# A graph transformer layer and a GAT layer: new start, constants as columns, last pair finished by quarters

## The chip, the cores and the metric

The kernel runs on one core of one Trainium2 chip. The metric is the device time of one execution in microseconds (us). A profiled execution gives a span, from the first to the last instruction, and the records of every engine. TensorE does matrix products into PSUM, VectorE and ScalarE work on rows of 128 partitions, GpSimd (POOL) does a few small operations, and SyncE (SP) issues most DMA transfers. Each engine takes its own instructions in order.

## The reference

There are 128 graphs (batches) of 128 nodes with 512 features, an adjacency matrix `adj` for each, and two layers, all in float32:

```
# layer 0: attention, 8 heads of 64
h = relu(layernorm(x))
q, k, v = h Wq^T + bq, h Wk^T + bk, h Wv^T + bv
attn = softmax((q k^T / 8) * (adj + adj))
x = x + (attn v) Wo^T + bo
# layer 1: graph attention
h = relu(layernorm(x))
Wh = h W ;  e = leaky_relu(Wh a1 + (Wh a2)^T, 0.2)
att = softmax(where(adj > 0.5, e, -9e15), axis=1)
x = x + elu(att Wh)
```

Here a1 and a2 are the two halves of the vector `a`.

## The kernel before

Graphs go in pairs: 64 pairs, numbered p from 0. Projections q, k and v are made for groups of two pairs (four graphs), and so one pair's steps carry half of the projection products of a later group. Every large product with a weight is written as seven smaller ones in place of eight (Winograd's form of Strassen's scheme): `PRODUCTS` lists, for each of the seven, the quarter of the activations, the quarter of the weights, and the PSUM bank (a, b or c). Weight tiles have seven slots: four quarters as loaded, and sums of quarters that `weight_sum` (steps Wv0 to Ww3) makes on VectorE. Products 0 and 1 use the loaded quarters 0 and 2; most others use sums. The token side has such sums too (`token_sum`: steps hs0 to hs3, cs, gs).

Work is divided into named steps, such as `lx` (load x of a pair), `t0`/`t1` (row statistics, lines 159 and 160), `pp` (reciprocal root on POOL, lines 163 and 164), `hn0`/`hn1` (normalised rows, line 181), `tp0`/`tp1` (turned by TensorE, line 188), `ev0`/`ev1` (ReLU into the hidden state, line 191), `U1` to `U11` (projection products, line 249), `F` and `A` (their evictions by ScalarE, lines 261 and 266, and additions by VectorE, line 270), `sca` to `plb` (scores, softmax, turned blocks that go out to memory and back), `o0` to `o6` and `w0` to `w6` (products with Wo and W, line 290), and `ez`, `fa`, `fb`, `so` (elu, addition, store: lines 476, 479, 482, 485). Three lists written out by hand give the order of the steps: `HEAD` for the first pairs, `ORDER` for each pair of the middle, `TAIL` for the last. Each list is one order over all engines; every engine takes its own instructions from it, in that order, DMA queues included. Pairs 0 to 3 turn their normalised rows on TensorE at the start; later pairs load x already transposed.

The first loads of `HEAD` are x of pair 0 in two halves, all of Wq (1 MB, `Lq`, line 622), x of pair 1, all of Wo and all of Wk. Before the lists begin, ScalarE's queue issues the biases bq, bk and bv as columns (`column`, line 107): 512 elements of 4 bytes each.

Two constants are made once. The row c is bo plus Wo applied to bv, minus 1, and is added to x of each pair (`sh`, line 225). It starts as a row bo that is spread over the partitions while it loads (`load_row`, line 120); `product_c` (line 494) makes the product with a broadcast column of bv on the one side and 256 columns of Wo on the other, so that the result stands on all partitions. The rows u_src and u_dst are W applied to a1 and a2: `dots_u` (line 507) makes columns by dot products on VectorE, `turn_u` spreads each with four transposes on TensorE, and `keep_u` copies it on ScalarE, u_src with the factor 1/MASK.

At the end, one exponential of 128x1024, two VectorE operations of 128x1024 and one store of 512 KB finish the last pair, as they do each pair.

Of the kernel before, what the change touches and what calls it, by code (L numbers as in the profile page):

```python
# [24 lines left out]
def kernel(  # L25
# [86 lines left out]
    bv_sb = column(bv, "bv")  # L112

# [3 lines left out]
    c_sb, us_sb, ut_sb = (const.tile([P, E], F32, name=name) for name in ("c", "u_src", "u_dst"))  # L117

    def load_row(dst, src, offset=0):
        nc.sync.dma_start(dst, bass.AP(tensor=src.tensor, offset=src.offset + offset, ap=[[0, P], [1, E]]))  # L120
# [32 lines left out]
    def row_stats(src, name):  # L153

        mv = small.tile([P, 2, 2], F32, name=name)

        def stats(i):
            st = small.tile([P, nc.vector.BN_STATS_DIM], F32, name="st")
            nc.vector.bn_stats(st, src[:, i, :])  # L159
            nc.vector.bn_aggr(mv[:, i, :], st)  # L160

        def power():
            nc.gpsimd.tensor_scalar_add(mv[:, :, 1], mv[:, :, 1], EPS)  # L163
            nc.gpsimd.tensor_tensor(mv[:, :, 1], mv[:, :, 1], mhalf.to_broadcast([P, 2]), OP.pow)  # L164

        return mv, stats, power
# [4 lines left out]
    def stats0(p, i):  # L171
        if p not in st0:
            st0[p] = row_stats(xs[p] if p < 3 else x0s[p], "mv0")
        st0[p][1](i)
# [234 lines left out]
    def dot1(p, i, k):  # L409
        h2, ws = h1s[p]  # L410
        junk = work.tile([P, E], F32, name="junk")
        nc.vector.scalar_tensor_tensor(  # L412
            junk, h2[:, i, :], 1.0, (us_sb, ut_sb)[k], op0=OP.mult, op1=OP.mult, accum_out=ws[:, i, k : k + 1]
        )
# [58 lines left out]
    def elu(p):  # L473

        ezs[p] = work.tile([P, 2, E], F32, name="ez")
        nc.scalar.activation(ezs[p], zs[p], AF.Exp)

    def finish_a(p):
        nc.vector.scalar_tensor_tensor(xs[p], zs[p], 0.0, xs[p], op0=OP.max, op1=OP.add)

    def finish_b(p):
        nc.vector.scalar_tensor_tensor(xs[p], ezs.pop(p), 1.0, xs[p], op0=OP.min, op1=OP.add)
# [4 lines left out]
    ucol = const.tile([P, 2, C], F32, name="ucol")  # L487


    def product_c():  # L490
        onces["c"] = pm = ps1.tile([P, 2, E // 2], F32, name="pm", tag="ps1")
        for f in range(2):
            for c in range(C):
                nc.tensor.matmul(  # L494
                    pm[:, f, :], bv_sb[:, c : c + 1].to_broadcast([P, P]), wo_sb[:, 2 * (c // 2) + f, c % 2, :],
                    start=(c == 0), stop=(c == C - 1),
                )

    def sum_c():
        pm = onces["c"].rearrange("p f k -> p (f k)")  # L500
        nc.vector.scalar_tensor_tensor(c_sb, pm, -1.0, c_sb, op0=OP.add, op1=OP.add)


    def dots_u(i, half):
        junk = work.tile([P, E], F32, name="junk")
        for c in (2 * half, 2 * half + 1):
            nc.vector.scalar_tensor_tensor(
                junk.rearrange("p (f k) -> p f k", f=2), w1_sb[:, 2 * half : 2 * half + 2, c % 2, :], 1.0,
                (us_sb, ut_sb)[i].rearrange("p (f k) -> p f k", f=2), op0=OP.mult, op1=OP.mult,
                accum_out=ucol[:, i, c : c + 1],  # L510
            )

    def turn_u(i):
        onces["u", i] = pu = ps1.tile([P, C, P], F32, name="pu", tag="ps1")
        for c in range(C):
            nc.tensor.transpose(pu[:, c, :], ucol[:, i, c : c + 1].to_broadcast([P, P]), ident)

    def keep_u(i):
        pu = onces["u", i].rearrange("p c k -> p (c k)")
        nc.scalar.activation((us_sb, ut_sb)[i], pu, AF.Copy, scale=1.0 if i else 1.0 / MASK)  # L520
# [11 lines left out]
    def listed(text, mark):  # L532
# [3 lines left out]
        lx@0 Lq@0 t0@-5 lx@1 Lo@0 Lk@0 Wq0@0 t1@-5 pp@0 t1@-4 lx@2 Lc@0 t0@-4 hn0@0 pp@1 Lv@0 hn1@0 tp0@0 Lw@0 tp1@0  # L536
        Lu0@0 ev0@0 hn1@1 ev1@0 hn0@1 tp1@1 Wq1@0 U6@-2 Wq2@0 tp0@1 ccp@0 ev0@1 t0@-3 F6@-2 t1@-3 ev1@1 Wk0@0 pp@2 l0@-2
        Wk2@0 la@-1 lt@0 Wk1@0 U5@-1 Lu1@0 hs2@-3 Wv0@0 hn0@2 U8@-2 ccd@0 hs0@-3 sh@0 U3@-1 t1@-2 tp0@2 F3@-1 la@0 U1@-1
        t0@-2 hs1@-3 pp@3 hn1@2 U7@-1 hs3@-3 hn0@3 hn1@3 U10@-2 cu01@0 F7@-1 l0@-1 ev0@2 Ww0@0 tp1@2 Wo0@0 U9@-1 ev1@2
        A8@-2 F10@-2 cu11@0 U1@-2 F9@-1 A5@-1 sh@1 tp0@3 U2@-1 tp1@3 F2@-1 U10@-1 ev0@3 A2@-1 ev1@3 hs0@-1 U4@-1 F10@-1  # L540
        Wv1@0 Wq3@0 t0@-1 U3@1 F4@-1 Ww1@0 hs1@-1 sca@0 t1@-1 scb@0 ata0@0 l0@0 s0@-1 ata1@0 U6@-1 mxa@0 Ww3@0 exa0@0
        U2@-2 Wv2@0 exa2@0 exa3@0 U8@-1 F1@-2 rca1@0 Wo2@0 nma2@0 exa1@0 U1@0 A9@-1 Wk3@0 rca0@0 t0@0 nma1@0 U3@-2
        nma3@0 A2@-2 nma0@0 t1@0 U4@-2 F3@-2 fla@0 l0@1 s0@0 f0@0 atb0@0 bla@0 U5@-2 atb1@0 Wv3@0 mxb@0 U11@-1 F5@-2
        exb3@0 U7@-2 A11@-1 exb1@0 A5@-2 exb0@0 cu00@0 U6@0 f0@1 pla@0 hs2@-1 Wo1@0 U2@0 F6@0 rcb0@0 A6@-1 F7@-2 exb2@0
        U9@-2 F1@0 rcb1@0 nmb3@0 F3@1 U10@0 A9@-2 lT@1 nmb2@0 cu10@0 nmb1@0 lT@0 sup0@0 scb@1 sua0@0 nmb0@0 sca@1 F10@0
        flb@0 U7@1 ata0@1 blb@0 ata1@1 A2@0 U5@1 F7@1 mxa@1 U9@1 Wo3@0 exa0@1 hd0@0 plb@0 exa2@1 exa1@1 pca@0 hs3@-1
        t0@1 U3@0 pea@0 rca0@1 hd1@0 nma1@1 exa3@1 U1@1 F3@0 rca1@1 t1@1 nma0@1 nma2@1 l0@2 s0@1 U2@1 nma3@1 la@1 fla@1
        U5@0 F2@1 atb0@1 bla@1 F9@1 hd0@1 o0@0 atb1@1 o1@0 mxb@1 pcb@0 pla@1 U4@1 peb@0 exb3@1 cs0@0 od0@0 exb1@1 cs1@0
        U8@0 A2@1 exb2@1 A5@1 exb0@1 cs2@0 U6@2 F5@0 A8@0 t0@2 t1@2 U4@0 od1@0 rcb1@1 rcb0@1 Ww2@0 nmb2@1 U8@1 nmb0@1
        nmb3@1 nmb1@1 U6@1 F4@1 flb@1 F6@2 hd1@1 U10@1 blb@1 hs0@1 cs3@0 o2@0 F10@1 A6@1 pca@1 od2@0 hs1@1 plb@1 sca@2  # L550
        pea@1 o4@0 ata0@2 ata1@2 o3@0 f0@2 od4@0 l0@3 mxa@2 U7@0 lt@1 od4c@0 A9@1 sup1@0 o5@0 sua1@0 exa1@2 o0@1 od5@0
        exa2@2 o1@1 exa0@2 o6@0 od0@1 st0@0 pcb@1 od6@0 st1@0 peb@1 scb@2 exa3@2 od1@1 pw@0 U11@1 cs0@1 rca1@2 rca0@2
        hs2@1 nma0@2 cs1@1 nma1@2 A5@0 s0@2 o2@1 nma2@2 nm@0 nma3@2 U1@2 F7@0 fla@2 h20@0 U9@0 atb0@2 F1@2 bla@2 h21@0
        atb1@2 mxb@2 U3@2 lT@2 A9@0 exb3@2 d00@0 exb2@2 U10@2 d01@0 pla@2 F3@2 od2@1 exb0@2 cs2@1 U5@2 hs3@1 A11@1 la@2
        d11@0 U4@2 F5@2 hd0@2 exb1@2 rcb1@2 rcb0@2 d10@0 o4@1 nmb3@2 nmb1@2 U8@2 od4@1 nmb2@2 A5@2 nmb0@2 flb@2 o3@1
        pb@0 U2@2 cs3@1 blb@2 od4c@1 wm@0 pr@0 U7@2 m1@0 o6@1 F7@2 plb@2 e1@0 o5@1 sw@0 U9@2 od6@1 hd1@2 g0@0 od5@1
        st0@1 g1@0 ge0@0 st1@1 A2@2
# [12 lines left out]
        so@-8 w0@-7 F10@-5 A9@-5 pw@-6 w1@-7 hs1@-5 sca@-4 zc0@-7 ge1@-7 scb@-4 ata0@-4 lx@-5 nm@-6 pca@-5 ata1@-4  # L570
        h21@-6 gs0@-7 mxa@-4 pcb@-5 pea@-5 U6@-4 peb@-5 A6@-5 exa1@-4 gs1@-7 gs2@-7 exa3@-4 cs0@-5 hs2@-5 o0@-5 h20@-6
        o1@-5 exa0@-4 d01@-6 U3@-3 exa2@-4 wd1@-7 cs2@-5 rca1@-4 d10@-6 nma3@-4 w2@-7 d00@-6 F6@-4 rca0@-4 U8@-4 sh@-5
        nma0@-4 zc2@-7 nma2@-4 cs1@-5 cs3@-5 nma1@-4 U11@-5 od0@-5 F3@-3 fla@-4 U10@-4 atb0@-4 bla@-4 od1@-5 lt@-5
        atb1@-4 w4@-7 mxb@-4 F10@-4 o2@-5 exb2@-4 w3@-7 od2@-5 exb3@-4 pla@-4 A11@-5 o4@-5 zc4@-7 d11@-6 exb0@-4 o3@-5
        hs3@-5 exb1@-4 rcb1@-4 la@-4 U2@-3 gs3@-7 wd4c@-7 nmb3@-4 rcb0@-4 nmb2@-4 nmb0@-4 pb@-6 w6@-7 wm@-6 od4@-5 pr@-6
        w5@-7 wd6@-7 od4c@-5 U7@-3 m1@-6 la@-3 zc5@-7 nmb1@-4 F2@-3 flb@-4 sca@-3 ez@-7 A8@-4 blb@-4 scb@-3 o6@-5
        ata0@-3 F7@-3 fa@-7 e1@-6 o5@-5 U5@-3 ata1@-3 mxa@-3 U9@-3 fb@-7 exa2@-3 exa1@-3 sw@-6 so@-7 U4@-3 exa0@-3
        plb@-4 exa3@-3 rca0@-3 nma1@-3 pca@-4 rca1@-3 od6@-5 F9@-3 od5@-5 st0@-5 g1@-6 nma0@-3 lx@-4 st1@-5 nma3@-3
        g0@-6 ge1@-6 A5@-3 pw@-5 nma2@-3 U10@-3 F4@-3 fla@-3 ge0@-6 U8@-3 nm@-5 atb0@-3 bla@-3 h21@-5 gs0@-6 pea@-4
        atb1@-3 h20@-5 w0@-6 d10@-5 F10@-3 mxb@-3 w1@-6 o0@-4 zc0@-6 d11@-5 exb0@-3 pla@-3 U1@-3 gs1@-6 exb3@-3 d00@-5  # L580
        exb2@-3 sh@-4 lt@-4 pcb@-4 wd1@-6 rcb1@-3 gs2@-6 o1@-4 peb@-4 exb1@-3 cs0@-4 w2@-6 od0@-4 nmb2@-3 rcb0@-3 cs1@-4
        pb@-5 nmb3@-3 wm@-5 sca@-2 nmb0@-3 od1@-4 A9@-3 zc2@-6 w3@-6 nmb1@-3 d01@-5 o2@-4 flb@-3 w4@-6 cs2@-4 blb@-3
        ata0@-2 U11@-3 zc4@-6 pr@-5 wd4c@-6 od2@-4 A2@-3 U1@-4 m1@-5 gs3@-6 cs3@-4 ata1@-2 o4@-4 plb@-3 F1@-4 e1@-5
        w6@-6 od4@-4 mxa@-2 o5@-4 lt@-3 la@-2 wd6@-6 o3@-4 exa2@-2 w5@-6 exa1@-2 od4c@-4 sw@-5 o6@-4 A11@-3 zc5@-6
# [182 lines left out]
```

## Time and profile before

| | |
|---|---|
| median of three runs | 2367.38 us (2365.86 to 2367.5) |
| span of the profiled execution | 2365.8 us (its time: 2367.53) |
| TensorE busy | 2340.5 us, 99% |
| VectorE busy | 2006.5 us, 85% |
| ScalarE busy | 1437.9 us, 61% |
| POOL busy | 222.7 us, 9% |
| first TensorE instruction | 11.55 us after the start |
| bytes moved | 306.11 MB, mean 129 GB/s |

In the profile, a line of a group or of the order in time names the source line, the engine, the operation and the tiles (output, then inputs). "Idle before" is the time in which that engine had nothing to do just before it, with what ended it. PE is TensorE, PEld its loading of weights, DVE VectorE, ACT ScalarE, and SPq the issuing of DMA by SP. Matmul ends are modelled and overlap the next start, so paces are best read from start to start.

### The profile page before, as it was taken

To read this page: it belongs to the slowest core of one execution; us is meant where nothing else is said; L and a number is where in the kernel's file an instruction comes from. 1 tells how busy PE (TensorE), PEld (TensorE's weight loads), DVE (VectorE), ACT (ScalarE), POOL (GpSimd) and SP (SyncE) were. 2 spreads that over 40 slices of the span, in tenths; PEclk is the share of its full clock that TensorE was granted. 3 is DMA by queue.
4 is the path that set the end of the run, shared out by engine and by line. 5 is a ranking of instruction groups with operands and counts; after the bars stand their busy time and mean duration, and the time that the engine had idled before them with its cause. 6 is when DMAs were issued, how large, how long until landed. Compare 5 with 4: busy or idle time off the path is not lost.

```text
span 2365.8 us, 40912 instructions
## 1 busy us (share of the span) xinstructions
PE 2340.5 (99%) x14264; PEld 2060.4 (87%) x14264; DVE 2006.5 (85%) x4037; ACT 1437.9 (61%) x4811; POOL 222.7 (9%) x323
## 2 busy tenths in 40 slices
PE   8999999999999999999999999999999999999997
PEld 7888888888888888888888888888888888888886
DVE  7788888888888888888888888888888888888887
ACT  3656556665566665655665666556656566665764
POOL 1000110101101101011011010010110100101000
PEclk9999999999999999999999999999999999999999
DMA  5434445444544454445454454544554435544332
GB/s 180 122 113 126 134 124 138 131 125 134 133 126 134 134 134 126 125 134 134 125 134 134 134 129 121 140 128 125 134 141 127 132 119 141 131 129 119 121 114 85
DMA packets 255277, 306.11 MB, mean 129 GB/s; under 512 B 21856, under 2 KB 181600, under 8 KB 254432
## 3 DMA queue, kind: packets, MB, share of 16 engines
q1 hardware_dynamic: 251568, 303.37, 46.6%
q8 instruction: 113, 1.85, 0.3%
q14 instruction: 92, 0.75, 0.1%
q0 software_dynamic: 1920, 0.13, 0.1%
q10 hardware_dynamic: 1584, 0.01, 0.0%
HBM read 202.64 MB, written 100.79 MB: 128 GB/s over the span
## 4 chain that ended last, share of the span: by engine, by line
PE 98%; DVE 1%; issue 0%; DMA 0%; ACT 0%; POOL 0%; SPq 0%; DVEq 0%; ACTq 0%; POOLq 0%
PE acc_a L249 28%; PE row_a L290 23%; PE acc_c L249 14%; PE row_c L290 9%; PE acc_b L249 7%; PE sc L311 5%; PE pc L375 5%; PE pg L453 5%; PE pb L421 1%; DVE junk L412 0%; DMA wq<-in_wqT 0%; PE pt L188 0%; DVE st L159 0%; POOL mv L164 0%; PE pm L494 0%
## 5 line engine op out<-in xcount | busy, mean ns | idle before, releaser
L330 ACT ACTIVATE at<-at,nmx 128x128 f32<-128x128 f32 x1024 | 396.3, 392 | 12.1 <-DVE nmx L325 9.6
L467 ACT COPY z<-row_a 128x256 f32<-128x256 f32 x256 | 94.8, 370 | 431.2 <-PE row_a L290 307.5
L339 ACT ACTIVATE at<-at,rs 128x128 f32<-128x128 f32 x1024 | 323.6, 394 | 4.0 <-DVE rs L334 3.9
L290 PE MATMUL row_a<-w,gT 128*128 128x256 f32 x1280 | 319.5, 380 | 1.7 <-ACT z L467 1.4
L290 PE MATMUL row_a<-wo,cxT 128*128 128x256 f32 x1280 | 318.7, 380 | 0.3 <-DVE cxT L147 0.3
L290 PEld LDWEIGHTS row_a<-w,gT 128*128 128x128 f32 x1280 | 242.1, 190 | 37.1 <-ACT z L467 2.6
L290 PEld LDWEIGHTS row_a<-wo,cxT 128*128 128x128 f32 x1280 | 233.9, 190 | 27.9 <-DVE cxT L147 0.5
L163 POOL TENSOR_SCALAR mv<-mv 128x2 f32<-128x2 f32 x128 | 30.5, 239 | 2089.2 <-DVE mv L160 2054.8
L266 ACT ACTIVATE kT<-acc_a,bk 128x256 f32<-128x256 f32 x256 | 107.1, 471 | 164.4 <-PE acc_a L249 163.0
L266 ACT ACTIVATE qT<-acc_a,bq 128x256 f32<-128x256 f32 x256 | 106.4, 469 | 164.1 <-PE acc_a L249 164.1
L330 ACT ACTIVATION_READ_ACCUMULATOR at<-at,nmx 128x1 f32 x1024 | 194.9, 190 | 0.0
L159 DVE BATCH_NORM_STATS2 st<-x 128x6 f32<-128x512 f32 x256 | 174.6, 682 | 9.1 <-DMA x<-in_x 6.9
L389 DVE TENSOR_TENSOR x<-row_a,x 128x256 f32<-128x256 f32 x320 | 133.3, 417 | 47.7 <-PE row_a L290 39.3
L318 DVE SCALAR_TENSOR_TENSOR at<-sc,adj 128x512 f32<-128x512 f32 x256 | 169.9, 685 | 4.5 <-PE sc L311 2.0
L346 DVE STREAM_TRANSPOSE tr<-at 128x1024 f32<-128x1024 f32 x128 | 158.3, 1237 | 9.4 <-ACT at L339 8.4
L325 DVE TENSOR_REDUCE nmx<-at 128x8 f32<-128x1024 f32 x128 | 155.9, 1218 | 3.2
L164 POOL TENSOR_TENSOR mv<-mv,mhalf 128x2 f32<-128x2 f32 x128 | 145.5, 1137 | 10.6
L453 PEld LDWEIGHTS pg<-w,h 128*128 128x128 f32 x1024 | 133.5, 192 | 7.0 <-issue 0.7
L311 PEld LDWEIGHTS sc<-kT,qT 64*128 64x128 f32 x2048 | 119.7, 188 | 21.1 <-issue 20.2
L453 PE MATMUL pg<-w,h 128*128 128x128 f32 x1024 | 134.3, 275 | 0.1
L290 PE MATMUL row_c<-w,gT 128*128 128x256 f32 x512 | 131.6, 379 | 1.0 <-DVE z L471 1.0
L311 PE MATMUL sc<-kT,qT 64*128 64x128 f32 x2048 | 132.4, 279 | 0.0
(126 smaller groups left out, 4897.3 us busy)
## 6 DMA issues: line engine op xcount, KB each, us to landing
blocks<-tr SPq DMA_DIRECT2D x128, 512.0 KB, 2.9
aT<-blocks SPq DMA_DIRECT2D x512, 128.0 KB, 3.1
x<-in_x SPq DMA_DIRECT2D x123, 512.0 KB, 3.8
out<-x SPq DMA_DIRECT2D x64, 512.0 KB, 5.7
hA<-in_xT SPq DMA_DIRECT2D x120, 256.0 KB, 4.0
mr<-rows SPq DMA_DIRECT2D x60, 256.0 KB, 4.5
adj<-in_adj SPq DMA_DIRECT2D x64, 128.0 KB, 5.1
adjT<-in_adjT SPq DMA_DIRECT2D x64, 128.0 KB, 5.0
```

Source lines behind the costliest of these rows:

```text
L159: nc.vector.bn_stats(st, src[:, i, :])
L164: nc.gpsimd.tensor_tensor(mv[:, :, 1], mv[:, :, 1], mhalf.to_broadcast([P, 2]), OP.pow)
L249: nc.tensor.matmul(acc[:, m, :], lhsT, rhs, start=fresh and m == 0 and c == 0, stop=c == 1, skip_group_check=True)
L266: nc.scalar.activation(dst(t, f)[:, m, :], a[:, m, :], AF.Identity, bias=bias[:, j : j + 1])
L290: nc.tensor.matmul(acc, left[:, la, c, :], w[:, wb, c, :], start=n in (0, 3) and c == 0, stop=c == 1, skip_group_check=True)
L311: nc.tensor.matmul(sc[s][:, j, :], qT[r, j, cols], kT[r, j, cols], start=True, stop=True)
L318: nc.vector.scalar_tensor_tensor(ats[b][0][:, k * C : (k + 1) * C, :], scs[b][k], QSCALE, adjs[p][:, i : i + 1, :].to_broadcast([P, C, S]) ...
L325: nc.vector.tensor_reduce(nmx, at, AX.X, OP.max, negate=True)
L330: nc.scalar.activation(at[:, j, :], at[:, j, :], AF.Exp, bias=nmx[:, j : j + 1], accum_out=sums[:, j : j + 1])
L339: nc.scalar.activation(at[:, j, :], at[:, j, :], AF.Copy, scale=rs[:, j : j + 1])
L346: nc.vector.transpose(trs[b], at.rearrange("p h (j k) -> p j h k", k=Q))
L453: nc.tensor.matmul(pg[:, c, :], h1s[p][0][:, i, c * P : (c + 1) * P], wts[p][:, i, :], start=True, stop=True)
```

## The change

- Each weight is loaded in two halves (`load_weight`): quarters 0 and 2 first (`Lk0`), quarters 1 and 3 later (`Lk1`). `HEAD` loads x of pairs 0 and 1 first, then the first halves of Wk and Wv.
- `warm_up` gives TensorE 24 transposes of the identity matrix at the very start.
- For pairs 0 to 3 (`soon`), the addition of EPS moves from POOL to VectorE, one 128x1 instruction for each row block.
- `bo` is a fourth column on ScalarE's queue. `product_c` makes c as a column of 128x4: 16 matmuls with one column each. `sum_c` adds bo and -1. `send_columns` stores the column to memory (POOL's queue) and `fetch_rows` loads it back as a row spread over all partitions (SP's queue). u goes the same way, in place of `turn_u` and `keep_u`; the factor 1/MASK moves into the dot products. Both halves of `a` load in one transfer.
- The last pair is finished by quarters of 128x256: steps `qe`, `qa`, `qb` in place of `ez`, `fa`, `fb`, and three stores `qs0` (256 KB), `qs1` and `qs2` (128 KB each).
- `HEAD` and `TAIL` are new lists; `ORDER` is the same.

```diff
+    bo_sb = column(bo, "bo")
...
+    def load_weight(w, src, k):
+        nc.sync.dma_start(w[:, 0:4].rearrange("p (j k) c f -> p j k c f", k=2)[:, :, k], src.rearrange("p (j k) c f -> p j k c f", k=2)[:, :, k])
...
+            if soon:
+                nc.vector.tensor_scalar_add(mv[:, i, 1:2], mv[:, i, 1:2], EPS)
...
     def product_c():
-        onces["c"] = pm = ps1.tile([P, 2, E // 2], F32, name="pm", tag="ps1")
-        for f in range(2):
+        onces["c"] = pm = ps1.tile([P, C], F32, name="pm", tag="ps1")
+        for j in range(C):
+            ms = slice(j % 2 * P, (j % 2 + 1) * P)
             for c in range(C):
                 nc.tensor.matmul(
-                    pm[:, f, :], bv_sb[:, c : c + 1].to_broadcast([P, P]), wo_sb[:, 2 * (c // 2) + f, c % 2, :],
+                    pm[:, j : j + 1], wo_sb[:, 2 * (c // 2) + j // 2, c % 2, ms], bv_sb[:, c : c + 1],
                     start=(c == 0), stop=(c == C - 1),
                 )
...
-    def turn_u(i):
-        onces["u", i] = pu = ps1.tile([P, C, P], F32, name="pu", tag="ps1")
-        for c in range(C):
-            nc.tensor.transpose(pu[:, c, :], ucol[:, i, c : c + 1].to_broadcast([P, P]), ident)
...
+    def send_columns(col, name):
+        onces[name] = d = dram.tile([col.shape[1], C, P], F32, name=name)
+            nc.gpsimd.dma_start(d.rearrange("i c p -> p i c"), col)
+    def fetch_rows(name, dst):
+        load_rows(dst, onces[name].rearrange("i c p -> (i c p)"))
+    def warm_up():
+        pu = ps1.tile([P, P], F32, name="warm", tag="ps1")
+        for _ in range(24):
+            nc.tensor.transpose(pu, ident, ident)
...
     HEAD = """
-        lx@0 Lq@0 t0@-5 lx@1 Lo@0 Lk@0 Wq0@0 t1@-5 pp@0 t1@-4 lx@2 Lc@0 t0@-4 hn0@0 pp@1 Lv@0 hn1@0 tp0@0 Lw@0 tp1@0
+        lx@0 lx@1 Lk0@0 Lv0@0 lx@2 la@-1 Lk1@0 Lq0@0 t1@-5 t0@-5 t0@-4 pp@0 t1@-4 hn0@0 pp@1 hn1@0 tp0@0 hn1@1 tp1@0
+        ev0@0 hn0@1 tp1@1 ev1@0 tp0@1 U3@-1 ev0@1 ev1@1 t1@-3 U1@-2 t0@-3 F3@-1 l0@-2 Lq1@0 pp@2 Lv1@0 Wk0@0 Lw0@0 U5@-1
+        F1@-2 Wk2@0 hs0@-3 hs1@-3 U2@-2 Wk1@0 hs2@-3 hn0@2 U6@-2 A5@-1 A2@-2 U7@-1 Wq0@0 t1@-2 U8@-2 t0@-2 F7@-1 F6@-2
...
     TAIL = """
...
-        ge1@-1 ez@-2 gs2@-1 w1@-1 gs0@-1 gs1@-1 w3@-1 zc0@-1 wd1@-1 fb@-2 w2@-1 gs3@-1 zc2@-1 so@-2 w4@-1 zc4@-1 w5@-1
-        wd4c@-1 w6@-1 zc5@-1 wd6@-1 fa@-1 ez@-1 fb@-1 so@-1
+        w1@-1 gs2@-1 gs0@-1 gs1@-1 w3@-1 gs3@-1 zc0@-1 wd1@-1 qa00@-1 w2@-1 fb@-2 zc2@-1 qe00@-1 so@-2 w4@-1 so@-3
+        zc4@-1 w5@-1 wd4c@-1 qb00@-1 qe11@-1 qa11@-1 w6@-1 qb11@-1 zc5@-1 qe01@-1 qa01@-1 qs1@-1 wd6@-1 qb01@-1 qe10@-1
+        qa10@-1 qs0@-1 qb10@-1 qs2@-1
```

In the new `TAIL`, the blocks of the last pair's attention (`flb`, `blb`, `plb`, `pcb` of -1) are separated by `o5@-2 o0@-1 o1@-1 o6@-2 g0@-3 g1@-3 w0@-3 w1@-3` on TensorE; in the old one by `o6@-2 pca@-1 o5@-2 o0@-1 o1@-1 w2@-3 w3@-3`.

## The prediction

> **What bounds the kernel now.** I read the page's busy shares and chain first, then stretches of both ends, then the instructions of those ends in order.
>
> ```profile
> PE 2340.5 (99%) x14264; PEld 2060.4 (87%) x14264; DVE 2006.5 (85%) x4037; ACT 1437.9 (61%) x4811; POOL 222.7 (9%) x323
> PE 98%; DVE 1%; issue 0%; DMA 0%; ACT 0%; POOL 0%; SPq 0%; DVEq 0%; ACTq 0%; POOLq 0%
> ```
>
> TensorE is busy 2340.5 of 2365.8 us and is 98% of the chain that ended last. So the change can win in two ways only: TensorE work that disappears or runs faster, and a share of the 25.3 us in which TensorE sits idle. The stretches say where those are (columns: stretch, its length, then busy us and instructions of PE, PEld, DVE, ACT, POOL, then clock, DMA share, GB/s):
>
> ```profile
> 0.00:15.00 15.00, 3.45 (x14) 3.09 (x15) 7.06 (x15) 2.48 (x3) 2.93 (x11) 1.00 0.87 317
> 15.00:30.00 15.00, 15.00 (x69) 13.01 (x69) 11.36 (x22) 2.65 (x6) 3.12 (x4) 1.00 0.74 253
> ...
> 2300.00:2320.00 20.00, 19.09 (x130) 16.38 (x129) 18.92 (x43) 15.51 (x50) 1.03 (x1) 1.00 0.36 122
> 2320.00:2340.00 20.00, 17.86 (x112) 14.70 (x111) 17.63 (x46) 6.96 (x17) 2.99 (x3) 1.00 0.35 103
> 2340.00:2350.00 10.00, 8.19 (x41) 5.84 (x40) 8.02 (x22) 5.72 (x14) 0.83 (x1) 1.00 0.00 1
> 2350.00:2360.00 10.00, 7.32 (x32) 5.19 (x31) 6.07 (x10) 4.24 (x8) 0.00 (x0) 1.00 0.27 105
> ```
>
> 11.55 us are idle at the start, then nothing for 2290 us, then about 5.9 us in gaps after 2300 (0.9 + 2.1 + 1.8 + 1.0), and 7.4 us after the last matmul. The repeated ORDER list is unchanged and has no gap to win. The first TensorE instructions, in order (start, duration):
>
> ```profile
> 11.55 2.82 PE L188 MATMUL pt<-ident,hn 128*128 128x128 f32 x12 [11.55 <-DVE hn L181]
> 14.21 3.45 PE L249 MATMUL acc_a<-hA,wq 128*128 128x256 f32 x8
> 17.49 0.60 PE L188 MATMUL pt<-ident,hn 128*128 128x128 f32 x4
> 17.93 3.62 PE L494 MATMUL pm<-wo,bv 128*128 128x256 f32 x16
> 21.38 1.89 PE L249 MATMUL acc_b<-hA,wk 128*128 128x256 f32 x8
> ```
>
> From start to start, 12 transposes take 2.66 us (222 ns each) and the first product 3.28 us; later four transposes take 0.44 us (110 ns) and a product 1.73 us. TensorE begins at half pace, although the clock column says 1.00 throughout. The bias product pm costs 3.46 us.
>
> **What the Trainium skill says.** "TensorE: Matmul & The Clock Gate", Part 1, says that TensorE's default state is throttled and that about 3.4 us of sustained activity, seen by a free-running window, releases it; an idle window brings it back. This trace agrees in kind: full pace came near 17 us, 5.4 us after the first transpose. "DMA: Bandwidth & Descriptors", Queues, rings and completion order, says that each DMA engine serves the queues that have work in turn, one packet at a time. The trace agrees: the 4-byte packets of the bias columns bq, bk, bv (ScalarE's queue) beside the large loads of SP landed near 4.4, 9.1 and 15.5 us. SP pays for it:
>
> ```profile
> SPq L622 <- DMA bv<-in_bv: 5.4, 1, 5.4
> SPq L72 <- DMA bk<-in_bk: 3.9, 1, 3.9
> SPq L622 <- DMA bq<-in_bq: 1.4, 1, 1.4
> ```
>
> In order of issue, wo, x of pair 2 and wv each began only when a bias column had landed; the DMAs between them did not wait. That fits a reuse of eight completion counters, dealt out alternately to ScalarE's and SP's first DMAs (my inference). With a fourth column, bo, the same dealing makes Lk0 wait for bq, the load of pair 2 for bk, Lk1 for bv and the load of pair 3 for bo, each with everything behind it on SP.
>
> **Start.** In before, x's first half is there at 3.81, but VectorE's queue then holds the first weight sum, which waits for the whole 1 MB of wq until 7.87; the second half's statistics start at 8.48. In after, x of pairs 0 and 1 are the first four loads and no weight sum stands ahead of the statistics. Bytes moved in before reach the 0.5 MB of pair 0 at about 4.4 us, so I take it landed at 4.9 (bounds 3.8 and 5.7). Four statistics at 0.88 us plus the new 128x1 add, 0.1 us as for other tiny VectorE instructions, are 3.9: 8.8 us. POOL's power (0.71 to 1.13 us) runs beside the statistics of pair 1. One row normalisation (0.52): first transpose at 9.4. The four normalisations run at 0.46 to 0.52, so the last transposes end near 11.3, and there the first product starts: pair 0's evictions (ScalarE, 0.60 each) are then done. In before the first product started at 14.21 with four transposes (0.44) still to come. Gain 2.9 + 0.44 = 3.3; bounds 2.5 and 4.4.
>
> **Warm clock.** identity is ready at 1.30 us; 24 warm-up transposes at 222 ns end near 6.8, beside the wait for x, so they cost nothing. If they release the clock and it holds over the 2.6 us to 9.4, the first product takes 1.73, not 3.28: gain 1.55 (bounds 0 and 1.55; -1.7 more if the second product is slow too). The transposes' own slow pace is in the start's sum.
>
> **Constants.** pm changes from 16 matmuls of 256 columns to 16 of one column. No row shows one column: above, at 190 ns (duration of one 128x128 weight load), it is 3.0 us; below, 0.05 us each, 0.8. Four transposes need 110 ns each with such weight loads, so I take 1.75: gain 1.7. The two turns of u (x4, L516, 0.44 each) go: gain 0.88. What replaces them is DMA: two small stores from POOL, two fetches on SP. The similar row stores (rows, POOL) took 6.1 us to land, the fetches (mr) 4.5. The lists put over 20 steps between store, fetch and use, so I take nothing; If the fetch of c is late, VectorE waits at the shift of pair 0, with a token normalisation (hd0) and accumulator additions (A9, later od0) queued behind it, for which TensorE's next banks wait: 0 to 2 us, mostly under the products already issued. On SP the fetches stand behind the block stores and loads and ahead of f0 and la of pair 2, which lead by tens of us. One broadcast of 512 KB instead of two of 256 KB, and 0.77 MB more fetched, run at a DMA share near 0.4.
>
> **Weights.** The first four products (k0, v0, k1, v1) use quarters 0 and 2, the first halves. By alternation, a column of 33 packets per engine beside 2 KB packets takes 33 x 114 ns = 3.8 us (bv beside 4 KB packets: 6.4 us, 194 ns each; minus 80 for 2 KB less): bk at 8.2, bv at 12.0, bo near 15. wv's 1 MB took 4.9 us, of which 2.5 are bytes; so k's second half lands at about 16.2, q's first at 18.0, q's second at 20.8, v's second at 22.1. TensorE ends the four products at 11.3 + 6.9 = 18.2 and needs q's first half: just there. Weight sums and token sums for k2 (six VectorE operations at 0.60) end at 19.8, needed at 19.9. The v2 sums end at 28.5, needed at 28.5. SP's load for pair 4 waits for the rows of pair 3 (one buffer), near 27 us; behind it stand the second halves of w1 and wo and adj of pair 1, needed only by the bias product and sums after 38: hidden. Three ties: I take 1.0 us of new waits; bounds 0 and 4.3, the latter with bv at 15.5 and bo at 20.
>
> Head: 3.3 + 1.55 + 1.7 + 0.9 - 1.0 = 6.5 us.
>
> **End.** In before:
>
> ```profile
> 2358.38 0.42 DVE L471 TENSOR_TENSOR z<-row_c,z 128x256 f32<-128x256 f32 x1 [1.63 <-PE row_c L290]
> 2358.90 1.06 ACT L476 ACTIVATE ez<-z 128x1024 f32<-128x1024 f32 x1 [1.01 <-DVE z L471]
> 2358.91 1.23 DVE L479 SCALAR_TENSOR_TENSOR x<-z,x 128x1024 f32<-128x1024 f32 x1
> 2360.24 1.23 DVE L482 SCALAR_TENSOR_TENSOR x<-ez,x 128x1024 f32<-128x1024 f32 x1
> ```
>
> From the last matmul to the store's issue: 3.1 us. By quarters only the add and three operations of 256 columns (0.41) remain behind the last matmul, pitch below 0.4: 1.5 to 1.6. The last store is 128 KB, not 512: 1.0 us less at the 390 GB/s seen there. Issuing the store of row block 0 (0.4) fits under the last two operations. Gain 2.5 (bounds 1.5 and 3).
>
> **Tail list.** The longest gap before 2340 is the last pair's context waiting 1.6 us for its reloaded blocks. TensorE work between flb and pcb of the last pair is 6.1 us in the old list (six row products at 0.86, one pc at 0.97) and 6.9 in the new one (six, and two gathers at 0.88). I take 0.8 gained and the rest even, since the closing dependencies of one pair stay; bounds -2.5 and +3.
>
> Sum 6.5 + 2.5 + 0.8 = 9.8 us: a span of 2356.0. The profiled run's time is 2367.53 for its 2365.8 span, beside a median of 2367.38; so 2357.6, rounded to 2357.5.
>
> **Rivals.**
> - Starved head: the columns land as late as in before, waits of 4.3 us: gain 6.5, 2361. For it: SP's waits above and a fourth column. Against: less traffic stands beside them.
> - The warm-up doesn't do what it says: window missed, or lost in the gap: 1.6 us or slightly more returns, 2359. Speaking for it: 5.4 us of work were needed before, and 5.3 are offered.
> - The tail list closes nearly all gaps: 2353.5. Against it: VectorE is busy 18.9 of 20 us there.
> - Slower: bo gates pair 3's load, the second halves of q and v behind it, and through VectorE's queue all later sums. It has slack until about 18 us; each us later is a us of TensorE. It eats the whole 10.8 us of gains when bo lands after 29, over 0.2% slower after 33.5. From 15.5 one more column at 6.4 gives 22, so it's unlikely.
>
> **How the numbers follow.** Forecast 0.55 (own range 2355 to 2360), starved head 0.18, no warm-up 0.12, better tail 0.10, slower 0.05. About 0.2%, 4.7 us, is what a measurement can tell from no change. The first, third and fourth and some six tenths of the starved case are beyond it: faster 0.88, same 0.07, slower 0.05. Range 2352.5 to 2363 leaves out the slower case and the edges of the others.
>
> **What would show it.** First hn transpose near 9.4, first product near 11.3 and lasting 1.73; pm near 1.75; no L516 turns; TensorE gaps between 11 and 32 us under 1.5 in all; from last matmul to end 4.9, not 7.4. Wrong if gaps on weights exceed 4 us, if a new VectorE wait for c or u stops TensorE, or if gaps after 2290 exceed 8.

## The result and the profile after

The changed kernel is slower: a median of 2378.62 us (2376.44 to 2379.87, four runs) against 2367.06 us, a ratio of 1.0049 with a 95% interval of 1.0031 to 1.0066. The forecast was 2357.5 us, in a range of 2352.5 to 2363. The profiled execution has a span of 2376.1 us, 10.3 more than before.

The page of the changed kernel, busy time and chain:

```profile
PE 2345.7 (99%) x14296; PEld 2066.1 (87%) x14296; DVE 2007.8 (84%) x4051; ACT 1441.2 (61%) x4812; POOL 221.8 (9%) x321
PE 97%; DMA 1%; DVE 1%; ACT 1%; SPq 0%; issue 0%; DVEq 0%
```

TensorE is busy 5.2 us more, most of it the warm-up (4.33 us). A new thing stands in the chain: DMA, 1%, or over 20 us. The stretches (same columns as before: PE, PEld, DVE, ACT, POOL, clock, DMA share, GB/s) say where:

```profile
0.00:15.00 15.00, 9.69 (x46) 9.12 (x47) 8.73 (x24) 3.57 (x5) 3.31 (x10) 0.77 0.89 272
15.00:30.00 15.00, 15.00 (x71) 13.22 (x70) 12.11 (x24) 3.00 (x7) 1.14 (x2) 1.00 0.39 139
...
60.00:80.00 20.00, 20.00 (x116) 17.48 (x115) 16.93 (x37) 11.95 (x45) 4.22 (x7) 1.00 0.59 54
80.00:100.00 20.00, 5.12 (x38) 4.30 (x37) 2.65 (x5) 2.83 (x7) 0.90 (x1) 0.57 0.92 140
```

The same two stretches of before:

```profile
60.00:80.00 20.00, 20.00 (x129) 17.27 (x128) 15.70 (x30) 14.37 (x54) 0.00 (x0) 1.00 0.53 146
80.00:100.00 20.00, 20.00 (x105) 17.30 (x104) 14.91 (x27) 11.73 (x42) 1.70 (x3) 1.00 0.47 112
```

Between 80 and 100 us TensorE works 5.12 us, where it worked all 20 in before. The DMA engines are busy 0.59 and 0.92 of these two stretches and move 54 and 140 GB/s; in before they were busy 0.53 and 0.47 of them and moved 146 and 112 GB/s. Most plainly in the first of them, the engines are held, not loaded: they are busy for longer and move less. The clock fell too, to 0.57 in the mean of the second stretch, so TensorE's first work after the gap ran at half pace (0.50 up to 100 us). The first TensorE instructions, and the bias product:

```profile
1.36 4.33 PE L543 MATMUL warm<-ident 128*128 128x128 f32 x24 [1.36 <-POOL ident masks.py:199]
9.64 3.67 PE L197 MATMUL pt<-ident,hn 128*128 128x128 f32 x16 [3.95 <-DVE hn L190]
13.11 2.68 PE L258 MATMUL acc_a<-hA,wk 128*128 128x256 f32 x8
15.63 1.89 PE L258 MATMUL acc_a<-wv,hA 128*128 128x256 f32 x8
...
47.15 3.63 PE L512 MATMUL pm<-bv,wo 128*128 128x1 f32 x32
```

And what TensorE waited for over the whole run (total, times, longest):

```profile
PE pc L384 <- DMA hA<-in_xT: 14.9, 1, 14.9
PE pt L197 <- DVE hn L190: 4.0, 1, 4.0
PE row_a L299 <- DVE z L480: 2.1, 2, 1.9
```

The context product pc doesn't read hA; hA's landing is only the last event that the profile sees before it. What pc reads is aT, the reloaded blocks. The DMA issues of 60 to 100 us (times, KB each, median us to landing) show that nearly everything issued there landed late, next to two small stores. First the changed kernel, then before:

```profile
blocks<-tr SPq DMA_DIRECT2D x2, 512.0 KB, 9.8
aT<-blocks SPq DMA_DIRECT2D x8, 128.0 KB, 13.7
...
crow<-ccol POOLq DMA_DIRECT2D x1, 2.0 KB, 14.5
urow<-ucol POOLq DMA_DIRECT2D x1, 4.0 KB, 15.0
```

```profile
aT<-blocks SPq DMA_DIRECT2D x12, 128.0 KB, 3.0
blocks<-tr SPq DMA_DIRECT2D x3, 512.0 KB, 3.5
```

The stores of the two columns were issued at 68.06 and 80.62 us; one reload of aT was 23 us under way. In the packets of the trace, those of 4 KB that began between 73 and 76 us took about 2 us each; such a packet of a block store takes about 0.16 us otherwise.

### The profile page after: what moved, and what is told of

The parts are those of the page before. It is cut to its first block, busy times and chain, and to the rows that moved or that the text cites. A ratio compares the mean times of both kernels' runs of the same rounds, so it can differ in the third digit from the quotient of the medians.

```text
span 2376.1 us, 41025 instructions
## 1 busy us (share of the span) xinstructions
PE 2345.7 (99%) x14296; PEld 2066.1 (87%) x14296; DVE 2007.8 (84%) x4051; ACT 1441.2 (61%) x4812; POOL 221.8 (9%) x321
## 4 chain that ended last, share of the span: by engine, by line
PE 97%; DMA 1%; DVE 1%; ACT 1%; SPq 0%; issue 0%; DVEq 0%
PE acc_a L258 28%; PE row_a L299 23%; PE acc_c L258 14%; PE row_c L299 9%; PE acc_b L258 7%; PE sc L320 5%; PE pc L384 5%; PE pg L462 5%; DMA aT<-blocks 1%; PE pb L430 1%; DMA hA<-in_xT 0%; PE pt L197 0%; ACT at L348 0%; DMA x<-in_x 0%; PE pm L512 0%
## 5 line engine op out<-in xcount | busy, mean ns | idle before, releaser
L421 DVE SCALAR_TENSOR_TENSOR junk<-h,u 128x512 f32<-128x512 f32 x256 | 176.2, 688 | 9.2 <-ACT h L414 1.8
L384 PE MATMUL pc<-aT,v 128*64 128x128 f32 x2048 | 128.5, 278 | 16.9 <-DMA hA<-in_xT 14.9
L320 PEld LDWEIGHTS sc<-kT,qT 64*128 64x128 f32 x2048 | 119.8, 188 | 21.6 <-issue 21.4
L384 PEld LDWEIGHTS pc<-aT,v 128*64 128x64 f32 x2048 | 112.0, 138 | 27.3 <-issue 19.0
```

The costliest lines, as they stand in the source:

```text
L320: nc.tensor.matmul(sc[s][:, j, :], qT[r, j, cols], kT[r, j, cols], start=True, stop=True)
L384: nc.tensor.matmul(pc[s * D : (s + 1) * D, j, :], vs[b // G][:, b % G, head * D : (head + 1) * D], aT[:, :, s * C + j, :], start=True, sto ...
L421: nc.vector.scalar_tensor_tensor(junk, h2[:, i, :], 1.0, u_sb[:, k, :], op0=OP.mult, op1=OP.mult, accum_out=ws[:, i, k : k + 1])
```

## The experiments

Theory A: the column stores hold the DMA engines. Theory B: the new `HEAD` brings SP's loads together and puts the reload late. Both can be true in part. "Median" below is the timed one; where a figure is from one profile, the text says so.

**The constants as rows again, the rest as changed.** The last two lines are a summary, the steps that leave `HEAD` and those that come in.

```diff
-                    pm[:, j : j + 1], wo_sb[:, 2 * (c // 2) + j // 2, c % 2, ms], bv_sb[:, c : c + 1],
+                    pm[:, f, :], bv_sb[:, c : c + 1].to_broadcast([P, P]), wo_sb[:, 2 * (c // 2) + f, c % 2, :],
...
-        ccs@0, cch@0, sus@0, suh@0
+        Lc@0 (bo as a row), sup0@0 sua0@0, sup1@0 sua1@0
```

> The changed kernel with only the way of the two constants undone: c and u become rows by TensorE again (16 matmuls of 256 columns, eight transposes), no column store and no fetch; bo is also loaded as a row, its column stays. Theory A (the stores of 4-byte elements hold the DMA engines from about 68 to 95 us, so that the block reload of pair 0 lands late and TensorE idles 14.9 us): the gap goes, a reload of blocks lands in 3 to 5 us, first store of out about 171 us in place of 187.6, time about 2361 to 2363. Theory B (the new list bunches SP's loads of x, adj, transposed x and blocks near 66 to 72 us, whatever POOL does): a gap of 8 us or more stays, time 2372 or more.

Median 2368.60 us, ratio 1.0002 (0.9994 to 1.0011). The 14.9 us wait is gone, and 10 us of time with it. But 5 us or more of the expected gain are missing: in its profile pc still waits for aT for 3.8 us in the head, and the runs spread from 2364.3 to 2371.2. They fall in two groups by their mean granted clock: five at 0.999 took 2364.3 to 2366.9, seven at 0.996 or 0.997 took 2368.5 to 2371.2. The profile is one of the first group, so it doesn't show what the others lost.

**The same stores, issued by SP.**

```diff
-            nc.gpsimd.dma_start(d.rearrange("i c p -> p i c"), col)
+            nc.sync.dma_start(d.rearrange("i c p -> p i c"), col)
```

> The changed kernel with the two column stores issued by SP instead of POOL; elements and places in the list are the same. Theory A (elements of 4 bytes are the cost, whoever issues them): the gap stays, within some us of 15, and large packets near the stores take over 1 us each. Theory C (POOL's queue is the cost[...]): the gap shrinks below 5 us, time about 2364 or less.

One run, 2375.99 us. TensorE's waits between 60 and 200 us come to 9.6 us in four pieces (two for aT, 5.9 together, the longer 5.2; one for x of 2.2; one for at of 1.5), in place of one of 14.9, near which Theory A had expected it to stay. In this one run the cost moved and stayed; the issuing queue isn't its cause.

**Columns turned to rows before they are stored.**

```diff
-            nc.gpsimd.dma_start(d.rearrange("i c p -> p i c"), col)
+        nc.tensor.transpose(pr, col.rearrange("p i c -> p (i c)"), ident)
+        nc.scalar.copy(rows, pr)
+        nc.gpsimd.dma_start(d.rearrange("i c p -> (i c) p"), rows)
```

> The changed kernel with each column first turned by one transpose on TensorE into rows of 128 and copied by ScalarE; POOL then stores 4 or 8 rows of 512 bytes; the fetches stay. Theory A: no gap, time about 2361 to 2363 (0.3 us of TensorE more, 0.9 less than turning u on all partitions). Theory B (bunched loads) or a cost of the fetches that spread a row over all partitions: a gap of 8 us or more stays.

Median 2367.49 us, ratio 0.9998 (0.9989 to 1.0006), 11 us below the changed kernel with the fetches in place. The fetches are therefore not the cost. As with the rows, some 5 us of the expected gain don't come.

**The kernel before with one column store added**, 1024 elements of 4 bytes that nothing reads.

```diff
+        d = dram.tile([2, C, P], F32, name="extra")
+            nc.gpsimd.dma_start(d.rearrange("i c p -> p i c"), ucol)
```

> The kernel before with one column store of 1024 elements of 4 bytes added on POOL's queue after u is ready, near 70 us; nothing reads it. Theory A: block reloads and loads around it take 10 us or more instead of 3 to 5, large packets take over 1 us, and TensorE gets a gap of 2 to 12 us where the reloaded blocks are used: 2369 to 2379. Theory B: nothing changes, 2367.

Median 2373.09 us, ratio 1.0022 (1.0015 to 1.0028): 5.3 us for one store of 4 KB. The profile is of the shortest of twenty runs, 2369.27 us; it has one new wait of TensorE, 1.8 us. DMA issues of 68 to 82 us in its profile:

```profile
blocks<-tr SPq DMA_DIRECT2D x1, 512.0 KB, 10.9
extra<-ucol POOLq DMA_DIRECT2D x1, 4.0 KB, 12.3
```

**The same, its elements 64 bytes apart in memory.**

```diff
-        d = dram.tile([2, C, P], F32, name="extra")
-            nc.gpsimd.dma_start(d.rearrange("i c p -> p i c"), ucol)
+        d = dram.tile([2, C, P, 16], F32, name="extra")
+            nc.gpsimd.dma_start(d.rearrange("i c p k -> p i c k")[:, :, :, 0], ucol)
```

> e1_before_plus_store with its 1024 elements of 4 bytes written 64 bytes apart in memory in place of side by side. Theory A1 (the cost is the number of small writes): the store lands in some 12 us again, block stores beside it take about 10 us, time 2371 to 2374. Theory A2 (neighbours in one line of memory wait for one another): landing near 4 us, packets of 4 KB at 0.16 us, time 2367 to 2368.5.

Median 2367.78 us, ratio 1.0000 (0.9992 to 1.0008): the cost is gone. The block store of the same stretch in its profile:

```profile
blocks<-tr SPq DMA_DIRECT2D x1, 512.0 KB, 3.9
```

Count, size, queue and time of the elements are the same; only their places differ. The expectation called this Theory A2, and its forecast holds: small writes side by side in memory are what costs. The places differ in two ways, however: the elements are no longer neighbours, and they spread over 64 KB in place of 4. Which of the two counts was not tried.

**The changed kernel with both column stores apart.** The fetches read bo in place of the stored columns, so no fetch waits for its store here.

> The changed kernel with both column stores writing their elements 64 bytes apart in memory; lists, queues and counts of elements are the same. Nothing reads the stored columns: the two fetches bring rows of bo in their place (u and c are left without their values). Theory A2 (small writes side by side in memory wait for one another and hold the DMA engines): no gap over 4 us near 80 us, packets of 4 KB near 0.2 us, time 2365 to 2369, as with columns turned first. Rival (in the changed kernel it is something else in the stores or their timing): a gap of 10 us or more stays, 2374 or more.

Median 2368.39 us, ratio 1.0001 (0.9995 to 1.0008), 10.2 us below the changed kernel. DMA issues of 60 to 100 us in its profile:

```profile
aT<-blocks SPq DMA_DIRECT2D x12, 128.0 KB, 5.4
hA<-in_xT SPq DMA_DIRECT2D x4, 256.0 KB, 4.9
blocks<-tr SPq DMA_DIRECT2D x2, 512.0 KB, 6.4
...
urow<-ucol POOLq DMA_DIRECT2D x1, 4.0 KB, 4.9
```

The kernel with turned columns, whose fetches do read what was stored, comes to nearly the same time. So the step that made the kernel slower is settled in the changed kernel too. It leaves the question why the other 9.8 us of gain aren't there.

**The first reload ahead of the load of transposed x, columns as changed.**

```diff
-  U1@0 lT@0 ... U3@0 pla@0 mxa@1
+  U1@0 pla@0 lT@0 ... U3@0 mxa@1
```

> The changed kernel with one step moved: the first reload of blocks (pla of pair 0) ahead of the load of transposed x on SP; the column stores and the 24 warm-ups stay. Theory A (the column stores hold up whatever SP moves from 68 us on): the first context product goes on time, the second, whose reload comes after the store of c, still waits 6 to 13 us; time 2370 to 2376. Rival (the order on SP alone is the cause): no gap over 3 us, 2362 to 2365.

Median 2380.03 us, above the 2370 to 2376 expected. The order on SP doesn't help beside the column stores; pc now waits 14.0 us at the other graph's blocks:

```profile
PE pc L384 <- DMA aT<-blocks: 15.4, 2, 14.0
```

**No warm-up**, on the kernel with turned columns.

> The kernel with columns turned first (e1_turned_first), without the 24 warm-up transposes. Theory A (the warm-up releases the clock, but the idle 3.5 us before the first real transpose take it back, so the sixteen transposes still run at half pace and only the first products gain): the first products take over 3 us each until some 5.5 us of work are done, 1.5 to 3 us slower than e1_turned_first. Theory B (the warm-up does nothing that lasts): within 1 us of it.

Median 2367.93 us, 0.4 above its parent: nothing that these runs can tell. In its profile the first product takes 3.03 us and the second 1.73. The expected 1.5 to 3 us are a miss.

**52 warm-up transposes.**

```diff
-        for _ in range(24):
+        for _ in range(52):
```

> e1_turned_first with 52 warm-up transposes in place of 24, which reach to about 9.5 us. Theory A: no idle stretch before the turned rows; sixteen transposes take 1.8 us instead of 3.3, the first product starts near 11.6 instead of 13.1 and runs at full pace; 1 to 1.5 us faster in the span if no weight is late. Theory B: the first product starts at 13 or later.

The start does what was expected in the profile: sixteen transposes in 2.08 us and the first product at 11.81.

```profile
1.36 8.04 PE L547 MATMUL warm<-ident 128*128 128x128 f32 x52 [1.36 <-POOL ident masks.py:199]
9.73 2.25 PE L197 MATMUL pt<-ident,hn 128*128 128x128 f32 x16 [0.34 <-DVE hn L190]
11.81 1.89 PE L258 MATMUL acc_a<-hA,wk 128*128 128x256 f32 x8
```

The median, 2367.62 us (2361.89 to 2370.79), doesn't follow. The profile is of the shortest of the twenty runs, and in it pc waits 2.6 us near 80 us, 1.4 of them for aT. The others go with their mean granted clock: the six runs at 0.999 or above took 2361.9 to 2365.2, the eleven at 0.997 or below 2367.5 to 2370.8. The kernel without a warm-up shows where a clock can fall. Its profile, of the longest of its twelve runs, waits 3.0 us for aT near 85 us, and there the clock falls to 0.77 and 0.55 (columns as in the stretches above):

```profile
85.00:90.00 5.00, 2.20 (x23) 1.64 (x25) 1.55 (x2) 1.37 (x5) 0.53 (x1) 0.77 1.15 243
90.00:95.00 5.00, 5.00 (x24) 4.00 (x21) 3.92 (x5) 0.77 (x3) 0.00 (x0) 0.55 0.51 190
```

So what is won at the start is, in part, waited for near 80 us, where the reload sets the time, and in most runs a slower clock comes on top. That it fell at this place in the runs without a profile is likely, and not shown.

**The early reload with turned columns.** This kernel also has the 52 warm-ups, which the expectation leaves out; its parent is therefore the kernel just above.

> e1_turned_first with one step moved: the reload of the first graph's blocks (pla of pair 0) stands ahead of the load of transposed x on SP, which waits 13 us for a product. Theory A (what remains of the gap near 80 us is the order on SP: a reload that could go at 58 us goes at 71): the first context product waits for nothing, its gap of 1.8 us goes and most of the next one's 1.2: 2 to 3 us faster. Theory B (loads that crowd together after 67 us make it, whatever the order): the gaps stay over 2.5 us in all.

Median 2361.91 us, ratio 0.9976 (0.9968 to 0.9985), 5.7 us below that parent, where 2 to 3 were expected. No wait for aT is left in the head of its profile; one of 0.3 us remains of 2.6. The rest of the 5.7 seems to go with the clock: all thirteen runs have a mean of 0.998 or more. This is Theory B's part, hidden until the column stores were out of the way. In the changed kernel, `pla` stood behind `lT`, on which SP waited 11.5 us for the product that still read hA; the block store issued at 54.6 us was reloaded only at 71.0. But its profile shows something new in the head (stretch, length, PE, clock, DMA share, GB/s, then the order in time):

```profile
44.00:47.00 3.00, 3.00 (x26) 1.00 0.00 1
47.00:50.00 3.00, 3.00 (x18) 0.65 0.89 270
50.00:53.00 3.00, 3.00 (x8) 0.50 0.42 166
53.00:56.00 3.00, 3.00 (x11) 0.71 0.43 175
```

```profile
45.09 4.24 PE L512 MATMUL pm<-bv,wo 128*128 128x1 f32 x32
49.20 3.76 PE L258 MATMUL acc_a<-wv,hA 128*128 128x256 f32 x8
52.75 2.88 PE L258 MATMUL acc_c<-hA,wq 128*128 128x256 f32 x8
55.47 1.89 PE L258 MATMUL acc_a<-hA,wq 128*128 128x256 f32 x8
```

TensorE had no idle time, yet its clock fell to half behind the one-column product, and two products took 3.55 and 2.72 us in place of 1.73. The profiles of turned columns, of no warm-up and of the early reload beside column stores show such a fall too; the changed kernel's own and three others with this product don't. Of the eight profiles with the product of 256 columns none does.

**c by the product of 256 columns.** The kernel above, with the bias product of before and no store of c.

> e2_early_reload (52 warm-ups, early reload, u turned first) with c made by the product of 256 columns again, as in before, directly as a row: no one-column product, no store and fetch of c. Theory A (one-column products count as idle for the clock, which falls to half for some us after them in some executions): full pace after pm in every profile, median 0.5 to 2.5 us below e2_early_reload's 2361.9, less spread. Theory B (the clock fell there for another reason): the same 2362.

Median 2360.37 us (2359.59 to 2361.09), ratio 0.9969 (0.9957 to 0.9980), 1.5 below the kernel above and with less spread. The clock stays full from 40 to 60 us. The wide product costs no more: 3.46 us from start to start, where the narrow one of the changed kernel took 3.49.

**The two halves of the end, on the kernel before.** First the new `TAIL` with the finish by quarters, then the old `TAIL` with the finish by quarters.

> The kernel before with only the new TAIL list and the last pair finished by quarters; start and constants as before. Theory A (the end of the change pays as the trace of after shows, some 2.5 us from the first store of out on): 2364.5 to 2365.5, ratio about 0.9989. Rival (the end gains only because the head came later or otherwise): 2367.

> The kernel before with its own lists, but the last pair finished by quarters as in the change. Theory A (the finish itself is worth 2.5 us, and the new tail list costs some of it through a wait of 1.9 us on a VectorE addition): from last matmul to end 4.5 to 5 us in place of 7.4, time about 2365.2, below e2_before_new_tail's 2366.8. Rival (finish worth 1 us or less): 2366.5 to 2367.5.

Medians 2366.81 us (ratio 0.9996, 0.9987 to 1.0004) and 2364.82 us (0.9988, 0.9982 to 0.9995). The finish alone gives 2.9 us. The new list takes back about 2.0, and misses the 2364.5 to 2365.5 expected of it. TensorE's waits after 2290 us, first with the new list, then with the old:

```profile
PE row_a L290 <- DVE z L471: 2.2, 2, 1.9
PE pc L375 <- DMA aT<-blocks: 1.5, 1, 1.5
PE row_a L290 <- ACT z L467: 1.2, 3, 0.5
PE row_a L290 <- DVE x L389: 0.4, 1, 0.4
```

```profile
PE row_a L290 <- ACT z L467: 1.4, 3, 0.5
PE pc L375 <- DMA aT<-blocks: 1.4, 1, 1.4
PE pb L421 <- DVE junk L412: 1.1, 2, 0.9
PE row_c L290 <- DVE z L471: 1.0, 1, 1.0
PE row_a L290 <- DVE cxT L147: 0.3, 1, 0.3
```

The wait on pc that I counted on shortening stays at 1.5, and a new one of 1.9 us stands at a product with W. But the waits come to 5.3 us with the new list and 5.2 with the old, so their sum doesn't explain the 2.0. Behind the wait of 1.9 us the new list's profile has a stretch at a lower clock, where the old list's keeps 1.00:

```profile
2344.00:2348.00 4.00, 3.96 (x12) 2.87 (x11) 1.99 (x6) 1.95 (x7) 0.00 (x0) 0.57 0.01 2
```

Whether that is the cost stays open: two of the twelve runs with the new list have a mean clock of 1.000, and they took 2367.4 and 2367.7 us, no less than the others.

**All together, with the old list at the end.** Early reload, 52 warm-ups, wide product, u turned first, old `TAIL`, finish by quarters.

> e3_wide_product (52 warm-ups, early reload, c by 256 columns, u turned first) with the old tail list and the last pair finished by quarters. If the new tail list costs about 2 us against the old one, as e2_before_new_tail and e3_before_quarters say: 2358 to 2359, below 2360.4. If it does so only behind the old head: 2360 to 2361.

Median 2359.34 us, ratio 0.9965 (0.9953 to 0.9978): 8.5 us below the runs of the kernel before beside it, and 19 below the changed kernel. It beats both. The old list gives 1.0 us against the wide product with the new list, half of what it gave on the kernel before. The runs of the wide product again go with the clock: three at a mean of 1.000 took 2359.6 to 2359.7 us, as fast as the old list, and three at 0.999 took 2361.0 to 2361.1. Its profile, one of the latter, has a clock of 0.57 between 2339 and 2343 us.

## Why the prediction was wrong

- **The column stores (the step that failed).** "I take nothing" for "two small stores from POOL, two fetches on SP", with 0 to 2 us as bound. They cost 10.2 us (11.0 when each kernel is set against its own runs of before): I asked whether their own landing would be late, not what they do to other transfers. The sign of the result is theirs. The row stores of before were a hint: 256 elements of 8 bytes side by side, 6.1 us to land; in the trace of before, the 4 KB packets that began in the microsecond from 85, just behind such a store, took 2.4 us each. I quoted the 6.1 as a latency.
- **Start.** First transpose 9.64, forecast 9.4: right. First product 13.11, forecast 11.3: wrong, because I let VectorE set the pace of the sixteen transposes and they ran at half pace, 217 ns each.
- **Warm clock.** 24 transposes took 4.33 us, less than the 5.3 of the half pace, so the release came during them; then 3.95 idle us took it back, where I had counted 2.6. The trace has the clock at half from 8 to 14 us. That agrees with the Trainium skill, "TensorE: Matmul & The Clock Gate", Part 1, which has a window of about 3.4 us in both directions; a gap that near to it had to be bridged. First product 2.52 us, between the two paces.
- **One-column product.** 3.49 us, forecast 1.75 with a top of 3.0. I read the x16 of before as sixteen calls, but it was eight, each shown as two matmuls; the sixteen calls of the change show as 32, at 109 ns each, so the product is no cheaper than with 256 columns. Its effect on the clock was not foreseen.
- **Weights.** 1.0 us of waits forecast, none measured: after 13 us nothing stopped TensorE before 80. The waits of SP for bq and bk were there (1.6 and 0.3 us) and hid. The columns bk, bv and bo landed at 5.8, 6.9 and 7.2 us, where I had put 8.2, 12.0 and nearly 15: the packet for packet alternation with SP's loads, by which I priced them, did not set their time here. The starved head is refuted, and the named way to slower, bo's landing, too.
- **SP's order.** I counted VectorE's sums against the weights and found ties; I did not follow the block reload, which stood behind a wait on SP. The reload moved earlier gave 5.7 us once the stores were out of the way, some of it by way of the clock.
- **End.** From last matmul to end 4.5 us, forecast 4.9; finish 2.9, forecast 2.5: right. Tail list: forecast +0.8, measured a loss of about 2.0, or 1.0 behind the new head. The count of TensorE work between two steps did not decide: the wait on pc hardly moved (1.6 to 1.5 us). A new wait on a VectorE addition came in, with a lower clock behind it; what each costs stays open.

Put together, the terms are these: stores 10.2, reload 5.7, start and first product 2.6, product pm 1.7, tail list 2.8, less 1.0 for weights and 0.4 for the finish, make 21.6 us. Forecast and result lie 21.4 apart, when each is taken from the median of before beside it (-9.8 and +11.6). The 5.7 was measured on the longer warm-up, however, and so may hold the 2.6 of the start in it; the sum is then 19.0. It holds changes of the clock as well, which no term of the forecast has. The single terms say more than that the sums lie close.

## What to carry to other kernels

Ask of a small transfer what it holds up, not only when it lands; turn a column into rows on TensorE before it goes to memory, or at least don't write its elements side by side one by one. When the head of a kernel gets faster, follow each reload through the queue that issues it: a reload behind a load that waits for a product is on the path as soon as TensorE arrives earlier. Try each list of an end alone: of the 2.9 us that the finish by quarters gained, the new list gave back about 2.0.

## What was not expected of the hardware

- 1024 writes of 4 bytes side by side in memory landed after 12.3 us and kept a block store of 512 KB for 10.9; 64 bytes apart, the block store took 3.9. The Trainium skill, "DMA: Bandwidth & Descriptors", Specifications, says that transfers below 512 bytes are read, modified and written; the runs show that smallness alone was not what cost, the placement was. That neighbours wait for one line of memory fits, and is not shown.
- One-column matmuls seem to count for little in what releases the clock: behind some 3.5 us of them the clock fell to 0.50 in four profiles of eight, with TensorE never idle, and in none of the eight with 256 columns. Why not in the others stays open; a free-running window, as the Trainium skill, "TensorE: Matmul & The Clock Gate", Part 1, has it, would explain that, and no run here tests it.
- Runs of one kernel differ in mean granted clock, and their times go with it: 2361.9 to 2365.2 us at 0.999 or above and 2367.5 to 2370.8 at 0.997 or below, with 52 warm-ups. The means don't say which comes first, a longer wait or a lower clock. One profile is one of these runs; a gain read from it need not be the gain of the median.
